# A planned Mamba and MLP kernel: joint silu groups, PSUM copies first, earlier fronts and new tie-breaks

## The chip, the cores and the metric

The kernel runs on one core of a Trainium2 chip. The metric is the device time of one execution in microseconds, as the median of several runs. The engines are TensorE (PE, with its weight loads as PEld), VectorE (DVE), ScalarE (ACT), GpSimd (POOL) and SyncE (SP), which here issues nearly all transfers between HBM and the on-chip memory SBUF. Matmuls write to PSUM, and another engine has to copy their results out.

## The reference

The input x is 8 samples of 384 channels by 32 x 32 pixels, so 1024 tokens of 384 channels per sample, all in float32. One layer has two halves:

```python
# for each of 8 samples, t: [1024, 384]
t  = layernorm(layernorm_over_channels(x))
xz = t @ in_proj_w.T                       # 384 -> 1536
xm, z = split(xz, 2)
xc = silu(causal_conv3(xm) + conv_b)       # 768 channels, 3 taps
dt, Bm, Cm = split(xc @ x_proj_w.T, [24, 40])
dt = softplus(dt @ dt_proj_w.T + dt_proj_b)
h_l = exp(dt_l * A) * h_{l-1} + dt_l * xc_l * Bm_l     # state: 768 x 16
y_l = (h_l . Cm_l) + xc_l * D
t  = (y * silu(z)) @ out_proj_w.T          # 768 -> 384
t  = gelu(t @ mlp_w1.T + b1) @ mlp_w2.T + b2           # 384 -> 1536 -> 384
x  = x + t
# then a feed-forward part on samples 0 to 4 (one group each of five)
h  = gelu(quant(layernorm(x) @ sign(W1 - mean).T + b1))
x  = x + quant(h @ sign(W2 - mean).T + b2)
```

`quant` scales a sample to 8 bits by its largest magnitude and clips it. The weights of the feed-forward part are binarised by groups of output features. For samples 5 to 7 that part is zero.

## The kernel before

**Tiling.** Features stand on the 128 partitions and tokens run along the free axis, in two halves of 512 (`HALVES`). For each sample there are four stages, written as functions of the class `Layer`:

- `s1(b)` is called the front. It loads x, normalises it (`norm`), projects it to xc (`p_in`, 6 x 3 matmuls per half), adds the three taps of the convolution from PSUM, applies silu, makes `p_dbc`, `p_all` and `p_dt`, applies softplus to dt, multiplies dt and xc, stores xc, dt, their product and B, C to HBM, and last projects the gate z (`p_z`) and applies silu to it (`gate`).
- `s2(b)` is the scan. Twelve tiles per sample, each with 4 groups of 4 states: ScalarE makes `da` = exp(dt A) into one of two PSUM buffers, GpSimd multiplies the input by B (`u<-dtx_r,bc`), VectorE runs the recurrence (L967), GpSimd or VectorE multiplies by C, and TensorE sums over states (`py`, L907). Samples 0 and 7 are scanned by halves, the others whole.
- `s3(b)` is the out-projection (`p_out`) and the MLP (`p_h`, gelu, `p_o`), per half.
- `ffn(b)`, for samples 0 to 4, is the binarised feed-forward part (`p_y`); `binarise` prepares its weights once.

**Buffers.** SBUF and PSUM tiles come from rings with a fixed number of buffers (L408 to L425). All matmuls but `py` write to the ring "mm" with three PSUM buffers. xc, z and dt of a front share the ring "front" with seven; the hidden layers share "hid" with nine.

**What sets the order.** No instruction is issued where it is written. `write_down` records operations with their costs, reads and writes in a `Plan`; `Plan.run` then plays a list scheduler: it keeps for each engine the time at which it is free, takes the engine that can start first, chooses one of its ready operations (`choose`) by rank (`rank`), emits it, and adds its cost. Each engine executes what it was given in that order, and semaphores between the engines follow from reads and writes. So the costs written in the code (`MM`, `c_act`, `c_dve`, the `cost` of each `add`, the `land` of a transfer) only set the order; on the chip, operations take what they take.

The rank (L295) puts `py` first (lane -1), then the scan (lane 0), then fronts of the samples up to `max(scanned + 1, FRONTS)` (lanes 1, 4, 11, 14), then the rest, then later fronts. On VectorE and GpSimd, stages go ahead of scans once they are ready (L287). Within a rank, the order of writing decides, shifted by up to 16 places through a hash (`turned`) of one number per 100 us of planned time from the table `TURNS` (L89).

ScalarE has a table of functions that must be loaded (`ACT_TABLE_LOAD`) before a function of another set. exp, silu, softplus and gelu need loads between them here; copies and scaled copies need none. `choose` stays with the loaded table as long as an operation of it is ready, unless it is exp (L283). To keep a function's operations together, the first operation of a group (`in_place`, L670; `gelu`, L1067) reads all tiles of the group, so none starts before all are there.

A copy out of PSUM (`affine`, L562) is planned on ScalarE, and VectorE may take it when it would start earlier. Where the planner sees TensorE idle for more than 0.7 us, it emits dummy matmuls `spare` of 128x256 (L350) as long as an "mm" buffer is free.

Of the kernel before, what the change touches and what calls it, by code (L numbers as in the profile page):

```python
# [33 lines left out]
P = 128  # L34
# [37 lines left out]
MM = 0.86  # L72
SWITCH = 0.26
BATCH = 2
# [3 lines left out]
EARLY = 2  # L78
FRONTS = 3
PATIENCE = 0.0  # L80
SLACK = 1.4
HOST = 0.3
NEAR = 1.0
LEAN = 1.1
LOAD_TABLE = 1.29


STRETCH, REACH = 100, 16
TURNS = (  # L89
    19522, 59978, 49910, 0, 34827, 0, 6565, 14275, 0, 7565, 33371, 19911,  # L90
    57895, 25116, 28986, 13399, 22123, 50761, 24784, 16788, 35300, 27386, 48162, 5457,
    0, 0, 40719, 11435, 20253, 0, 2806, 25936,
)


def turned(n, by):
# [3 lines left out]
    return (x ^ x >> 13) % (2 * REACH + 1) - REACH  # L100


def c_act(n):
    return 0.25 + n * 0.00084


def c_dve(n):
    return 0.19 + n * 0.00102


def c_pair(n):
    return 0.19 + n * 0.00188


def c_pool(n):
    return 0.18 + n * 0.00214

# [81 lines left out]
class Plan:  # L199
# [12 lines left out]
    def add(self, engine, cost, emit, r=(), w=(), claim=(), table=None, size=0, others=None,  # L212
            land=1.6):
        op = Op()
        op.engine, op.cost, op.emit, op.table = engine, cost, emit, table
        op.others, op.settle = others or {}, None
        op.size, op.land, op.prio = size, land, (*self.prio, len(self.ops))
        op.next, op.ready, op.tiles = [], 0.0, []
# [39 lines left out]
    def run(self):  # L258
# [7 lines left out]
        left, scanned = len(self.ops), 0  # L266

        def taken_by(op):
            return [t for t in op.tiles if t.ring is not None and t.real is None]
# [11 lines left out]
        def choose(e, now, able):  # L281
            able = [op for s, op in able if s <= now]
            if e == "ACT":  # L283
                same = [op for op in able if op.table == table and table != "exp"]
                plain = [op for op in able if op.table in (None, "exp")]
                able = same if table is not None and same else plain or able
            if e in ("DVE", "POOL"):  # L287

                able = [op for op in able if op.prio[0] > 0 and op.ready <= now - PATIENCE] or [
                    op for op in able if op.prio[0] == 0] or able  # L290
            at = int(now / STRETCH)
            turn = TURNS[at] if at < len(TURNS) else 0
            return min(able, key=lambda op: rank(op, turn))

        def rank(op, turn):  # L295


            lane, b = op.prio[:2]
            if lane <= 0:
                first = (lane, b)  # L300
            elif lane == 7:
                first = (EARLY, b)
            elif lane in (1, 4, 11, 14):
                first = (1, b) if b <= max(scanned + 1, FRONTS) else (3, b)
            else:
                first = (2, b)
            return (*first, op.prio[2] + (turned(op.prio[2], turn) if turn else 0))

# [12 lines left out]
        while left:  # L321
# [45 lines left out]
            if op.table is not None and op.table != table:  # L367
                cost += LOAD_TABLE
                table = op.table
            end = free[e] = clock.run(now, cost) if e == "PE" else now + cost  # L370
            if e == "SP":
                dma_free = max(dma_free, end + 0.5) + 0.05 + op.size / 360e3
                end = dma_free + op.land
# [17 lines left out]
class Layer:  # L391
# [115 lines left out]

    def load(self, to, view, src, r=(), size=0, cost=0.46, land=2.3):

        self.plan.add(  # L510
            "SP", cost, lambda: self.nc.sync.dma_start(view(to.real), src), r=r, w=[to],
            size=size, land=land,
        )
# [8 lines left out]
    def rows_moved(self, t, parts, move, r, w):  # L522
        n = P // len(parts)
        for i, mem in enumerate(parts):
            self.plan.add(
                "SP", 0.42, lambda i=i, mem=mem: move(t.real[i * n : (i + 1) * n, :], mem),
                r=r, w=w(i), size=4 * n * T,
            )

    def weights(self, ring, k, src, r=()):  # L530
        w = self.piece(ring, [P, k, P], ring)
        self.load(w, lambda t: t, src, r=r, size=4 * P * k * P, cost=0.37, land=1.5)
        return w
# [28 lines left out]
    def affine(self, out, in_, r, w, bias=0.0, scale=1.0, n=T, pool=False):  # L562
# [19 lines left out]
        if pool:  # L582
            others = {"POOL": (0.18 + n * 0.00095, on(nc.gpsimd))}
        else:
            others = {"DVE": (c_dve(n), on(nc.vector))}
        extra = 0.0 if plain else 0.09 if isinstance(scale, float) else 0.18
        self.plan.add("ACT", 0.16 + n * 0.00083 + extra, on_act, r=r, w=w, others=others)

    def norm(self, t, eps, scale):

        nc, add = self.nc, self.plan.add
        def columns(src, name):
# [10 lines left out]

            add("PE", 0.9, emit, r=[src], w=[p])
            return p

        def spread(src, name, turned=False):
# [29 lines left out]
        p_turned = self.piece("mm", [P, G], "p_turned")  # L637
        add("PE", 0.5, lambda: nc.tensor.matmul(
            p_turned.real, var.real, self.ident[:, ::DQ], start=True, stop=True
# [3 lines left out]
            r=[p_turned], w=[rstd])  # L643
        add("POOL", 0.8, lambda: nc.gpsimd.tensor_tensor(
            rstd.real, rstd.real, self.power.to_broadcast([P, G]), ALU.pow
# [8 lines left out]
    def s1(self, b):  # L654
# [14 lines left out]

        def in_place(t, func, table):  # L670
            parts = [t[k] for k in range(KD)]
            for p, piece in enumerate(t.pieces):
                mine = parts[p * PER : (p + 1) * PER]
                self.act(lambda piece=piece: piece.real, lambda piece=piece: piece.real, func,
                         c_act(PER * T), r=parts if p == 0 else mine, w=mine, table=table)
# [14 lines left out]
        def gate(half, t):  # L690
            z = self.split(r_z, KD, "z")
            for m in range(KD):
# [4 lines left out]
                )  # L697
            in_place(z, AF.Silu, "silu")
            by_pair("z", half, z)

        for half, cols in enumerate(HALVES):
# [4 lines left out]
            for m in range(KD):  # L706
# [12 lines left out]
                for s in (1, 2):  # L719
                    add("DVE", c_dve(T) + 0.06, lambda m=m, xc=xc, pm=pm, s=s, tap=tap: (  # L720
                        nc.vector.scalar_tensor_tensor(
# [4 lines left out]
            if half:  # L726
# [6 lines left out]

                add("POOL", 0.9, edge, r=[halo[m] for m in range(KD)], w=[self.edged])
                for p, piece in enumerate(xc.pieces):
                    add("POOL", 0.25, lambda p=p, piece=piece: nc.gpsimd.tensor_add(
                        piece.real[:, :, :2], piece.real[:, :, :2],
                        self.edge[:, p * PER : (p + 1) * PER, :2],
                    ), r=[self.edged], w=[piece[k] for k in range(PER)])
            all_m = [xc[m] for m in range(KD)]  # L740
            in_place(xc, AF.Silu, "silu")
            by_pair("xc", half, xc)


# [12 lines left out]

            add("PE", 0.26 + KC * MM, low, r=[w, *all_m], w=[p_dbc], claim=[dbc])
            self.affine(lambda dbc=dbc: dbc.real, lambda p_dbc=p_dbc: p_dbc.real, [p_dbc], [dbc])
# [12 lines left out]
            for k in range(0, KD, 2):  # L772
# [16 lines left out]
                for i in range(2):  # L789
# [3 lines left out]
                    )  # L793
            in_place(dt, AF.Softplus, "softplus")
            d = self.dram["dtx", b]
# [8 lines left out]
            for p, piece in enumerate(dt.pieces):  # L804
# [5 lines left out]
                )  # L810
            gate(half, t)

# [13 lines left out]
    def scan(self, b, half, state):  # L826
# [7 lines left out]

        def load(to, view, src, r, size):
            self.plan.add("SP", 0.57, lambda: nc.sync.dma_start(view(), src), r=r, w=[to],  # L836
                          size=size, land=2.3)

        def quad_rows(i):
            r = self.piece(f"bc{i}", [P, n], f"bc{i}")  # L840
            src = rows.real[i * SQ : (i + 1) * SQ, cols].unsqueeze(0).to_broadcast([DQ, SQ, n])
            load(r, lambda: r.real, src, [rows[h] for h in halves], 4 * P * n)
            return r
# [90 lines left out]
    def scan_pair(self, u, cols, n, dts, dtxs, bq, cq, state, half, on_pool):  # L934
# [14 lines left out]
        for t, mine in enumerate(cols):  # L949
            da = self.piece("da", [P, wide, n], "da")  # L950
            dt_r = dts[t]
            for i, col in enumerate(mine):
                self.act(
                    lambda i=i, da=da: da.real[:, i, :],
                    lambda i=i, dt_r=dt_r: dt_r.real[:, i, :], AF.Exp,
                    0.26 + n * 0.00084, r=[dt_r[i]], w=[da], table="exp",
                    scale=self.a_neg[:, col : col + 1],
# [43 lines left out]
    def s3(self, b):  # L1001
        nc, a, add = self.nc, self.a, self.plan.add
        yg_d = self.dram["yg", b]
        for half, cols in enumerate(HALVES):
# [12 lines left out]
            else:  # L1017
                yg = self.split("hid", KD, "yg")
                for p, piece in enumerate(yg.pieces):
# [5 lines left out]
                        w=[piece[k] for k in range(PER)], claim=yg.pieces[p:],  # L1025
                        size=4 * P * PER * T, land=2.3,
                    )
# [12 lines left out]
            for h in range(KH):  # L1040
# [5 lines left out]
                )  # L1046
                if h % HK == HK - 1:
                    self.gelu(g, h + 1 - HK)
            for m in range(KC):
                rows = slice(m * P, (m + 1) * P)  # L1050
                res = self.piece("res", [P, T], "res")

                self.load(res, lambda t: t, a["x"][b, rows, cols], r=[g[HK]], size=4 * P * T)
                po = self.mlp_out(lambda i, m=m: a["mlp_w2"][m, i], "w6", g, [res], "p_o")
# [11 lines left out]

    def gelu(self, g, k0, r=(), **kw):  # L1067
        parts = [g[k] for k in range(k0, k0 + HK)]
        for i in range(0, HK, PER):
            piece = g.pieces[(k0 + i) // PER]  # L1070
# [129 lines left out]
    def clip(self, view, n, parts, q):  # L1200
        self.plan.add("POOL", 0.13 + n * 0.0009, lambda: self.nc.gpsimd.tensor_scalar(
            view(), view(), q.real[:, 2:3], q.real[:, 1:2], ALU.min, ALU.max
        ), r=[q], w=parts)

    def ffn(self, b):
# [32 lines left out]
        for h, cols in enumerate(HALVES):  # L1238
            g = self.split("hid", KH, "gf")
            for p, piece in enumerate(g.pieces):  # L1240
# [3 lines left out]
                    r=[y1_d[h, p * PER + m] for m in range(PER)], w=parts,  # L1244
                    claim=g.pieces[p:], size=4 * P * PER * T, land=2.3)
                self.clip(lambda piece=piece: piece.real, PER * T, parts, q1)
# [135 lines left out]
```

## Time and profile before

| | |
|---|---|
| median of 3 runs | 3187.56 us (3181.11 to 3189.2) |
| the profiled execution | 3184.62 us, of which the span of instructions 3182.5 us |
| TensorE busy, idle | 3083.4, 99.1 us |
| dummy matmuls `spare` | 58.1 us (114 matmuls, two records each) |
| granted TensorE clock, mean | 0.988 |
| VectorE, ScalarE, GpSimd busy | 2644.0, 1966.5, 2744.8 us |
| table loads of ScalarE | 172 profiled (173 in the program), 1283 ns each |
| `p_h` matmuls | 1152 records for 576 matmuls of 128x512, 511.7 us busy |
| copies of 128x512 out of PSUM | 583 to 775 ns on ScalarE, 681 to 801 ns on VectorE |

How to read the rows that follow. A row of stretches gives first the stretch and its length, then busy microseconds and number of instructions of PE, PEld, DVE, ACT and POOL, then the granted clock, the busy share of the DMA engines and GB/s. A row of waits names the engine and instruction that waited, after the arrow the one that released it, and then the total in us, how often, and the longest. A row of a group names line, engine, operation, tiles, count, busy us and mean ns of one, and then the idle time of its engine just before it.

The span ends with 66 us in which only the MLP of the last half is left; before that the last scan has to be done. Sample by sample, the last `py` ends at 531, 917, 1301, 1664, 2035, 2395, 2755 and 3113 us.

### The profile page before, as it was taken

The numbers are of one execution on the slowest core, as the hardware profiler recorded it, in microseconds if no ns is written. First come the engines' busy times: TensorE is split into PE (matmuls) and PEld (weight loads), VectorE is DVE, ScalarE is ACT, GpSimd is POOL, SyncE is SP. The second block draws the span as 40 slices with busy tenths as digits, with TensorE's granted clock in tenths as the row PEclk, the third lists the DMA queues.
The fourth block names the chain that finished last, engine by engine and source line by source line (L and its number), as shares of the span: only waits on it lengthen the run. The fifth ranks groups of instructions, "written<-read, shape, count | busy, mean of one in ns | idle before, by whom it ended". The sixth has DMA issues, their size and how long they took to land. (4 is left out here: it accounts for less than half of the span.)

```text
span 3182.5 us, 33759 instructions
## 1 busy us (share of the span) xinstructions
PE 3083.4 (97%) x10972; PEld 1274.9 (40%) x10972; DVE 2644.0 (83%) x2081; ACT 1966.5 (62%) x2363; POOL 2744.8 (86%) x1046
## 2 busy tenths in 40 slices
PE   9898999999999999999999999999999999999999
PEld 4333434343433443433444434343434443433334
DVE  4697888899788798879998888889789987888881
ACT  4777786855665556665656655666566555655552
POOL 1788889988988978999979999799989999998980
PEclk9998999999989999999999999999999999999999
DMA  7797789757786667875696766877677856756542
GB/s 231 261 310 263 252 261 329 255 195 259 239 283 221 198 227 254 295 250 185 230 319 234 252 207 232 298 236 254 219 257 254 282 196 213 235 175 209 160 148 72
DMA packets 348975, 751.85 MB, mean 236 GB/s; under 512 B 36481, under 2 KB 113793, under 8 KB 339585
## 3 DMA queue, kind: packets, MB, share of 16 engines
q1 hardware_dynamic: 348368, 749.61, 71.0%
q8 instruction: 88, 1.44, 0.2%
q14 instruction: 87, 0.70, 0.1%
q10 hardware_dynamic: 432, 0.09, 0.0%
HBM read 569.21 MB, written 180.36 MB: 236 GB/s over the span
## 5 line engine op out<-in xcount | busy, mean ns | idle before, releaser
L942 POOL TENSOR_TENSOR u<-dtx_r,bc 128x2048 f32<-128x2048 f32 (+1 forms) x360 | 1185.5, 3308 | 124.9 <-PE py L907 79.7
L556 ACT ACTIVATE da<-dt_r,a_neg 128x1024 f32<-128x1024 f32 (+1 forms) x960 | 900.5, 945 | 490.0 <-DVE u L967 272.3
L942 POOL TENSOR_TENSOR u<-u,bc 128x2048 f32<-128x2048 f32 (+1 forms) x274 | 900.1, 3290 | 86.9 <-DVE u L967 81.4
L967 DVE TENSOR_TENSOR_SCAN u<-da,u 128x1024 f32<-128x1024 f32 (+1 forms) x436 | 869.1, 2007 | 127.1 <-POOL u L942 71.4
L540 PE MATMUL p_h<-t,w_b 128*128 128x512 f32 x1152 | 511.7, 597 | 10.8 <-DMA w_b<-in_mlp_w 6.8
L540 PE MATMUL p_o<-g,w 128*128 128x512 f32 x1152 | 512.6, 597 | 5.1 <-DMA w<-in_mlp_w 5.1
L967 DVE TENSOR_TENSOR_SCAN da<-da,dtx_r 128x1024 f32<-128x1024 f32 (+1 forms) x192 | 386.3, 2019 | 55.6 <-POOL dtx_r L942 34.2
L942 POOL TENSOR_TENSOR dtx_r<-dtx_r,bc 128x2048 f32<-128x2048 f32 (+1 forms) x120 | 396.8, 3311 | 2.4
L540 PEld LDWEIGHTS p_h<-t,w_b 128*128 128x128 f32 x1152 | 214.0, 190 | 298.0 <-issue 257.7
L540 PEld LDWEIGHTS p_o<-g,w 128*128 128x128 f32 x1152 | 214.3, 190 | 295.8 <-issue 277.9
L540 PE MATMUL p_y<-tn,w_b 128*128 128x512 f32 x720 | 319.6, 597 | 2.2 <-DVE tn L648 2.2
L540 PE MATMUL p_y<-gf,w_n 128*128 128x512 f32 x720 | 320.3, 597 | 0.8 <-ACT gf L556 0.5
L907 PE MATMUL py<-u,fold 128*32 128x512 f32 x2304 | 303.5, 628 | 0.2 <-POOL u L942 0.2
L967 DVE TENSOR_TENSOR_SCAN da<-da,u 128x1024 f32<-128x1024 f32 (+1 forms) x140 | 283.7, 2041 | 13.7 <-POOL u L942 6.9
L540 PE MATMUL p_out<-yg,w 128*128 128x512 f32 x552 | 245.6, 597 | 4.2 <-DMA w<-in_out_proj_last 1.5
L540 PE MATMUL p_z<-t,w_f 128*128 128x512 f32 x504 | 233.4, 610 | 9.2 <-DMA w_f<-in_in_proj_w 5.1
L540 PE MATMUL p_in<-t,w_f 128*128 128x512 f32 x504 | 229.7, 601 | 5.6 <-DMA w_f<-in_in_proj_w 3.7
L556 ACT ACT_TABLE_LOAD x172 | 220.7, 1283 | 3.1
L540 PEld LDWEIGHTS p_y<-gf,w_n 128*128 128x128 f32 x720 | 133.9, 190 | 185.3 <-issue 173.8
L540 PEld LDWEIGHTS p_y<-tn,w_b 128*128 128x128 f32 x720 | 134.0, 190 | 182.1 <-issue 165.1
L571 ACT ACTIVATE g<-p_h,v_vecs 128x512 f32<-128x512 f32 x158 | 107.7, 684 | 145.2 <-PE p_h L540 144.7
L571 ACT ACTIVATE y<-p_y,v_vecs 128x512 f32<-128x512 f32 x138 | 94.2, 684 | 166.9 <-PE p_y L540 139.0
(132 smaller groups left out, 3245.0 us busy)
## 6 DMA issues: line engine op xcount, KB each, us to landing
dt_r<-dt_d SPq DMA_DIRECT2D x144, 512.0 KB, 5.5
dtx_r<-dtx_d SPq DMA_DIRECT2D x72, 1024.0 KB, 6.0
w_b<-in_mlp_w SPq DMA_DIRECT2D x192, 192.0 KB, 3.1
w<-in_mlp_w SPq DMA_DIRECT2D x96, 384.0 KB, 3.5
w_f<-in_in_proj_w SPq DMA_DIRECT2D x168, 192.0 KB, 4.8
y_d<-y SPq DMA_DIRECT2D x120, 256.0 KB, 4.7
gf<-y_d SPq DMA_DIRECT2D x60, 512.0 KB, 6.9
xc_d<-xc SPq DMA_DIRECT2D x48, 512.0 KB, 5.6
```

The source lines that it names most:

```text
L540: self.nc.tensor.matmul(p.real, w.real[:, w0 + k, :], t.at(k0 + k), start=start and k == 0, stop=stop and k == n - 1,)
L556: lambda: self.nc.scalar.activation(out(), in_(), func, **{k: v() if callable(v) else v for k, v in kw.items()}),
L571: nc.scalar.activation(out(), in_(), AF.Identity, bias=bias, scale=scale)
L907: nc.tensor.matmul(py.real[g * DQ : (g + 1) * DQ, :], self.fold, hc, start=False, stop=(q == NQUAD - 1), skip_group_check=True,)
L942: nc.gpsimd.tensor_mul(u.real[:, x], t.real[:, x], row.real.unsqueeze(2).to_broadcast([P, n, 2]))
L967: da=da, in_u=in_u: nc.vector.tensor_tensor_scan(to(i), da.real[:, i, :], in_u(i), state.real[:, col : col + 1] if half else 0.0, ALU.mult ...
```

## The change

Five things change.

- **Joint silu.** For samples 2 to 7 (`JOINT`) the gate's projection is written right behind the convolution, and one group of silu covers xc and z: six operations, the first of which reads all twelve parts. The z stores follow the xc stores. For samples 0 and 1 the gate stays last.
- **gelu by eight and four.** In `s3`, the twelve hidden tiles get gelu in groups of 8 and 4 tiles where they had two of 6.
- **PSUM first.** When at most one buffer of "mm" is free (`SCARCE`), ScalarE chooses among the operations that touch one, if there are any that need no other table.
- **Fronts.** `FRONTS` is 4 where it was 3.
- **Costs, ties and flags.** Most costs are set anew, ScalarE and VectorE count as free 0.09 and 0.08 us before an operation's end (`LAG`), transfers get rates by kind. `TURNS` has 30 new numbers, and four bits of each may let fronts wait (`LATE_FRONTS`), scans go first on VectorE or GpSimd (`DVE_SCANS`, `POOL_SCANS`) or stages go first on ScalarE (`ACT_STAGES`) in that stretch of 100 us.

```diff
-SWITCH = 0.26
+SWITCH = 0.22
+JOINT = range(2, B)
-FRONTS = 3
+FRONTS = 4
+SCARCE = 1
+LATE_FRONTS, DVE_SCANS, POOL_SCANS, ACT_STAGES = 1 << 16, 1 << 17, 1 << 18, 1 << 19
 TURNS = (
-    19522, 59978, 49910, 0, 34827, 0, 6565, 14275, 0, 7565, 33371, 19911,
...
+    17610, 24087, 20212, 39788, 55575, 59023, 81989, 22321, 58617, 812894,
+    311620, 51673, 560357, 59520, 80314, 2104, 50573, 559844, 6159, 58063,
+    51278, 41401, 6390, 863060, 0, 672911, 34250, 39179, 27191, 131575,
 )
+LAG = {"ACT": 0.09, "DVE": 0.08}
 def c_act(n):
-    return 0.25 + n * 0.00084
+    return 0.2 + n * 0.00084
...
         def choose(e, now, able):
             able = [op for s, op in able if s <= now]
+            at = int(now / STRETCH)
+            turn = TURNS[at] if at < len(TURNS) else 0
             if e == "ACT":
                 same = [op for op in able if op.table == table and table != "exp"]
                 plain = [op for op in able if op.table in (None, "exp")]
                 able = same if table is not None and same else plain or able
+                if turn & ACT_STAGES:
+                    able = [op for op in able if op.prio[0] > 0 and op.table in (None, "exp")] or able
+                if len(self.spare.ring.free) <= SCARCE:
+                    able = [op for op in able if self.spare.ring in map(ring_of, op.tiles) and (
+                        op.table in (None, "exp", table))] or able
             if e in ("DVE", "POOL"):
-                able = [op for op in able if op.prio[0] > 0 and op.ready <= now - PATIENCE] or [
-                    op for op in able if op.prio[0] == 0] or able
+                scans = [op for op in able if op.prio[0] == 0]
+                if not (turn & (DVE_SCANS if e == "DVE" else POOL_SCANS) and scans):
+                    able = [op for op in able if (
+                        op.prio[0] > 0 and op.ready <= now - PATIENCE)] or scans or able
+                else:
+                    able = scans
...
             elif lane in (1, 4, 11, 14):
-                first = (1, b) if b <= max(scanned + 1, FRONTS) else (3, b)
+                soon = 2.5 if turn & LATE_FRONTS else 1
+                first = (soon, b) if b <= max(scanned + 1, FRONTS) else (3, b)
...
-            end = free[e] = clock.run(now, cost) if e == "PE" else now + cost
+            end = clock.run(now, cost) if e == "PE" else now + cost
+            free[e] = end - LAG.get(e, 0.0)
             if e == "SP":
-                dma_free = max(dma_free, end + 0.5) + 0.05 + op.size / 360e3
+                dma_free = max(dma_free, end + 0.4) + op.size
...
-            others = {"DVE": (c_dve(n), on(nc.vector))}
+            others = {"DVE": (c_dve(n) + (0 if isinstance(scale, float) else 0.15), on(nc.vector))}
...
-        def in_place(t, func, table):
-            parts = [t[k] for k in range(KD)]
-            for p, piece in enumerate(t.pieces):
+        def in_place(func, table, *ts):
+            parts = [t[k] for t in ts for k in range(KD)]
+            for p, piece in enumerate(piece for t in ts for piece in t.pieces):
...
-            in_place(xc, AF.Silu, "silu")
+            z = gate(half, t) if b in JOINT else None
+            in_place(AF.Silu, "silu", *([xc, z] if z else [xc]))
             by_pair("xc", half, xc)
+            if z:
+                by_pair("z", half, z)
...
-            gate(half, t)
+            if not z:
+                z = gate(half, t)
+                in_place(AF.Silu, "silu", z)
+                by_pair("z", half, z)
...
-                if h % HK == HK - 1:
-                    self.gelu(g, h + 1 - HK)
+                if h in (7, 11):
+                    self.gelu(g, 0 if h == 7 else 8, n=8 if h == 7 else 4)
```

The other hunks set costs of single operations (the norm's matmuls from 0.9 to 0.78, the clip from 0.13 + 0.0009 n to 0.2 + 0.00096 n, and the like).

## The prediction

> **What bounds the kernel now.** I read the page's busy shares first, then its slices, then the stretches of 100 us, then the waits, and last the length of each sample's scan.
>
> ```profile
> PE 3083.4 (97%) x10972; PEld 1274.9 (40%) x10972; DVE 2644.0 (83%) x2081; ACT 1966.5 (62%) x2363; POOL 2744.8 (86%) x1046
> ...
> PE   9898999999999999999999999999999999999999
> ...
> POOL 1788889988988978999979999799989999998980
> PEclk9998999999989999999999999999999999999999
> ```
>
> TensorE is busy for 97% of the span, so only what it loses can be won: 3182.5 - 3083.4 = 99.1 us idle; the dummy matmuls `spare`, 58.1 us; and the clock, granted at 0.988, so 0.012 x 3182.5 = 38 us. Together 195 us; some 2987 us are real work that the change leaves as it is. The stretches show where the loss lies (columns: stretch, its length, then busy us and instructions of PE, PEld, DVE, ACT, POOL, granted clock, DMA share, GB/s):
>
> ```profile
> 100.00:200.00 100.00, 86.70 (x323) 35.08 (x322) 86.75 (x88) 80.56 (x116) 93.00 (x66) 0.95 0.83 278
> 200.00:300.00 100.00, 80.56 (x316) 29.10 (x315) 85.67 (x93) 74.42 (x111) 85.09 (x57) 0.87 0.80 267
> ...
> 900.00:1000.00 100.00, 92.44 (x318) 37.59 (x317) 78.92 (x57) 63.13 (x71) 94.06 (x33) 0.90 0.75 250
> ...
> 2200.00:2300.00 100.00, 99.94 (x319) 39.01 (x318) 84.79 (x58) 64.18 (x70) 98.59 (x34) 1.00 0.76 250
> ```
>
> The first three stretches hold 12.4 + 13.3 + 19.4 = 45 us of the idle time, and the first four 23 us of the clock's loss. 900 to 1000 holds 7.6 and 10 us. From 1000 to 2700 TensorE loses 15 us in all, and GpSimd is nearly as full. The same by sample (from the first scan to the last `py` of each of the eight samples; samples 0, 2, 3, 6 are shown):
>
> ```profile
> 70.00:531.00 461.00, 416.31 (x1559) 169.35 (x1557) 376.05 (x376) 349.04 (x495) 388.94 (x230) 0.95 0.83 277
> ...
> 917.00:1301.00 384.00, 374.15 (x1333) 154.49 (x1330) 325.39 (x231) 231.53 (x262) 336.13 (x97) 0.97 0.72 239
> 1301.00:1664.00 363.00, 359.70 (x1284) 148.16 (x1283) 320.89 (x224) 215.18 (x238) 331.69 (x99) 1.00 0.73 246
> ...
> 2395.00:2755.00 360.00, 358.25 (x1239) 153.05 (x1238) 316.53 (x227) 211.01 (x230) 340.97 (x107) 1.00 0.71 236
> ```
>
> Sample 0 takes 461 us, samples 1 and 2 386 and 384, the later ones 358 to 371. GpSimd works 332 to 341 us of each of samples 3 to 6 and idles 19 to 31: there little can be won by any order. So there are two bounds, TensorE in the first 1300 us and both engines after it, and the gain has to come from samples 0 to 2.
>
> **The change, part by part.** No arithmetic changes: the new program has the same real matmuls, scans, products and 2255 DMAs; what differs is order, who empties PSUM, table loads (173 to 195) and dummies (114 to 109).
>
> *One silu group for xc and z (samples 2 to 7), gelu by eight and four.* The first should take ScalarE loads away: groups that start with z fall from 15 to 4. But `LAG` lets ScalarE choose 0.09 us before its last operation ends, and the second operation of a group depends on the end of the first, which read all its parts. At that moment it cannot be chosen, so an exp or a PSUM copy can slip in and split the group. The built order shows it: gelu loads 31 to 43, those that start with xc 16 to 20, softplus 16 to 19, feed-forward gelu 11 to 12, returns to exp 83 to 96.
>
> ```profile
> L556 ACT ACT_TABLE_LOAD x172 | 220.7, 1283 | 3.1
> ...
> DVE u L967 <- ACT da L556: 62.4, 47, 5.8
> ...
> DVE da L967 <- ACT da L556: 26.6, 22, 6.7
> ```
>
> By this row 22 loads are 22 x 1.283 = 28.2 us. The Trainium skill speaks against the change here: "ScalarE: Activation LUTs", What ACT_TABLE_LOAD costs, puts 1380 ns of drain beside the 1283 ns of each switch, and its Table sets section says to batch by set; 22 x 2.66 would be 58.5 us. The row shows 3.1 us of idle time before 172 loads, so no such drain; I take 28. ScalarE idles 3182.5 - 1966.5 = 1216 us, which hides most. What shows is VectorE waiting for exps: 62.4 + 26.6 = 89 us over 83 returns, 1.07 us each. 13 more returns give 14 us; VectorE is 83% busy and some of that is covered: +10 us, bounds 0 and 28. Queued behind a load on ScalarE stand the next exp, and behind that VectorE's scan, GpSimd's product and `py`. The split gelu wins nothing at the very end: in the chain 72 `p_o` follow 72 `p_h` without a gap. The joint group makes `p_dbc` wait for six more projections, 18 x 0.888 (511.7 us over 576 `p_h`, two records each) = 16 us later per half. Samples 2 to 7 stand well ahead of their scan, which hides it; without that cover a scan would start 16 us late. The z stores go before the `p_dbc` weights in SyncE's queue, three of 0.59 us (the issue of an xc store in the timeline): 1.8 us, under the same cover. Both 0.
>
> *PSUM emptied first.* With one or no "mm" buffer free, ScalarE prefers an operation that frees one. TensorE's own waits behind such copies:
>
> ```profile
> PE p_all L762 <- ACT dbc L569: 4.2, 1, 4.2
> ...
> PE p_dbc L752 <- ACT halo L569: 3.7, 1, 3.7
> PE p_dt L783 <- ACT dbc L569: 2.7, 3, 1.6
> PE p_mean L616 <- ACT mean L571: 2.6, 6, 0.5
> PE p_mean L616 <- ACT dt L571: 2.5, 2, 1.7
> PE p_in L540 <- ACT dt L571: 2.4, 3, 0.8
> ```
>
> With five smaller rows for copies of halo, dt, z, g and var (2.1, 2.3, 2.0, 2.1, 2.1) and `p_all` behind dbc on VectorE (1.5) this is 18.1 + 12.1 = 30 us. I take two thirds: -20 us, bounds 0 and -30. The copy that goes ahead delays an exp by its 0.58 to 0.68 us; scans then wait, already in the +10. ScalarE also takes over copies: 85 of 128x512 (z, dt, g, xc, y, t) are left on VectorE of 112. 27 x 0.74 = 20 us less on VectorE, 27 x 0.68 = 18 us more on ScalarE; both have idle time, 0.
>
> *Four early fronts.* In the order, by the last `py` of sample 0 TensorE has done 372 full 128x512 matmuls where it had done 344, and 38 dummies for 49. By sample 1 the lead is 39 matmuls, by sample 2 16, by sample 7 none. So 28 x 0.888 = 25 us of real work is drawn into the holes of sample 0, and taken out of sample 2. This is worth the holes that it fills. Of the 45 us idle before 300 us, about 15 are start-up data (first x, norm, the `p_sums` weights) that no order fills; PSUM-first already took about 15 there; I give this part the remaining 15: -15, bounds 0 and -20. Dummies: (109 - 114) x 0.51 (58.05 over 114) = -2.5. The clock follows idle time in this trace: each of the longer half-speed stretches in its record (131, 223, 250, 264, 295, 919 us) stands right behind waits. If the waits shrink by the above, I take 15 of the first 23 us and 5 of the 10 at 919: -20, bounds 0 and -33. If nothing is there to hide the front (the drawn work itself has to wait for its weights), it costs its 25 us in sample 0.
>
> *The planner's costs, ties and flags.* They only re-order. Waits for weights (`p_sums` 6.8, `p_h` 6.8, `p_o` 5.1, `p_z` 5.1, `p_in` 3.7 and 2.0, `p_out` 1.5 and 0.8) are 32 us; transfers are now costed finer, kind by kind. No row says how much better: bounds -20 and +10, taken -5. Flags let scans or stages go first, or fronts later, in nine stretches of 100 us: 0.
>
> *What is given back.* Where GpSimd is full, TensorE's saved time turns into waiting. The order carries as many dummies late (47 in samples 6 and 7 before, 51 after: 2 us). I take +8, bounds 0 and 25.
>
> Sum: +10 - 20 - 15 - 2.5 - 20 - 5 + 8 = -44.5 us. The profiled execution has a span of 3182.5 us and a time of 3184.6; the median of the runs is 3187.6, 5.1 above the span. Span 3138.0, so the time 3143 us.
>
> **The rivals.**
> - *Given back.* The early holes close, but samples 3 to 7 are set by GpSimd and cannot run faster than their 358 to 371 us, while exps come later: only samples 0 to 2 gain, 30 us, and 12 go again: 3170. For it: 19 us of GpSimd idle in samples 5 and 6. Against: 31 in samples 3 and 4.
> - *Deep gain.* Nearly all PSUM, weight and early waits go and the clock stays up: -30 - 20 - 33 - 15 - 2.5 + 10 = -90: 3097. For it: every term is idle time in the trace. Against: sample 1 carries more real work than before.
> - *Nothing happens.* The new order has its own waits of the same size, as its almost equal number of dummies suggests: 3187, within 0.3% (9.6 us, about what a measurement can tell).
> - *Slower: the table loads decide.* From sample 3 on, each extra return to exp stalls the loop exp, scan, product, as GpSimd has no slack: the whole 28 us, and the early gain stays under 15 us since the drawn fronts delay sample 0. It decides once a return costs over 2 us instead of 1.07 and the holes give less than that: 3187 + 28 - 5 = 3210. For it: more loads, and 62 us of VectorE waiting on exps. Against: most loads stand in ScalarE's 1216 us idle.
>
> **How the numbers follow.** Main case 0.50 (its own range 3115 to 3170), deep gain 0.17, given back 0.17, nothing 0.08, slower 0.08. Faster 0.50 + 0.17 + 0.17 = 0.84, same 0.08, slower 0.08. The range reaches from below the deep gain to just past "nothing": 3085 to 3190; it leaves out the slower case and the tail of the deep one.
>
> **What would show it.** TensorE's idle time from 99 to about 60 us, that of the first 300 us from 45 to about 20; granted clock from 0.988 to 0.994 or more; about 194 table loads and more VectorE waiting on `da`; the last `py` of sample 0 near 515 us, of sample 2 near 1265 (1301 before), samples 3 to 7 within 10 us of their lengths. Wrong would be: idle time over 85 us, a clock still at 0.988, or samples 3 to 7 longer by over 5 us each.

## The result, and the profile after

The changed kernel takes 3153.12 us in the median (3150.01 to 3154.6) beside 3188.38 us for the kernel before on the same chip: 35 us less, a ratio of 0.989 with a 95% interval of 0.9868 to 0.9911. The profiled execution has a span of 3152.0 us where it had 3182.5; that is 30.5 us less, where single executions of the kernel before lie between 3181.11 and 3193.61 us. One execution of the run `more_loads` was in a slow state (5717 us at a granted clock of 0.745), and all times below are of fast runs.

The page of the changed kernel, busy shares and slices:

```profile
PE 3073.8 (98%) x10962; PEld 1274.0 (40%) x10962; DVE 2602.0 (83%) x2056; ACT 2000.8 (63%) x2409; POOL 2747.2 (87%) x1047
...
PE   9989999999999999999999999999999999999999
...
POOL 1788888998999988999989999989998999988990
PEclk9999999999999999999999999999999999999999
```

TensorE is idle for 3152.0 - 3073.8 = 78.2 us (99.1 before) and its clock is granted at 0.992 in the mean (0.988), so the clock costs 0.008 x 3152 = 25 us (38). The dummies last 58.9 us, though there are five fewer (58.1). Taking the dummies out, TensorE is busy for 3073.8 - 58.9 = 3014.9 us where it was 3025.3, with the same 10744 records of matmuls: I put the 10.4 us down to the higher clock. So the 30.5 us of the span are 20.9 us of idle time and 10.4 us of clock, less 0.8 us of dummies.

The stretches of 100 us that stood out, in the changed kernel (the columns are those of the rows before the change):

```profile
100.00:200.00 100.00, 90.10 (x347) 36.31 (x346) 81.10 (x85) 83.01 (x115) 82.57 (x58) 0.97 0.88 296
200.00:300.00 100.00, 92.35 (x392) 37.61 (x391) 82.83 (x91) 84.72 (x125) 85.77 (x59) 0.95 0.89 299
...
900.00:1000.00 100.00, 99.55 (x383) 39.01 (x382) 86.50 (x58) 68.16 (x78) 96.79 (x27) 1.00 0.83 291
```

From 200 to 300 TensorE is busy for 92.4 us instead of 80.6 and its clock is at 0.95 instead of 0.87; from 900 to 1000 it is busy for 99.6 us instead of 92.4, and the slow clock there is gone. In the first 300 us 45 us of idle time became 28. By sample, with the ends of the last `py` of this trace:

```profile
70.00:550.00 480.00, 448.29 (x1727) 184.67 (x1729) 383.54 (x387) 382.12 (x541) 389.48 (x234) 0.98 0.86 287
550.00:929.00 379.00, 373.04 (x1422) 155.80 (x1414) 336.05 (x253) 245.70 (x285) 346.18 (x111) 1.00 0.74 252
929.00:1287.00 358.00, 353.46 (x1333) 146.26 (x1327) 318.76 (x232) 230.44 (x258) 331.26 (x99) 0.99 0.76 257
1287.00:1652.00 365.00, 361.59 (x1278) 148.27 (x1278) 311.36 (x217) 221.68 (x240) 340.68 (x102) 0.99 0.70 239
1652.00:2010.00 358.00, 356.60 (x1234) 145.17 (x1234) 310.88 (x223) 220.46 (x241) 336.61 (x105) 1.00 0.72 244
2010.00:2380.00 370.00, 367.41 (x1254) 149.78 (x1242) 316.03 (x229) 238.81 (x258) 340.15 (x105) 1.00 0.74 248
2380.00:2726.00 346.00, 342.05 (x1172) 144.97 (x1168) 298.62 (x209) 199.20 (x215) 337.44 (x103) 1.00 0.70 229
2726.00:3082.00 356.00, 343.25 (x1066) 136.99 (x1062) 294.13 (x263) 213.28 (x306) 315.69 (x176) 0.99 0.55 170
```

The samples of the kernel before that the prediction leaves out (1, 4, 5 and 7):

```profile
531.00:917.00 386.00, 375.25 (x1418) 154.10 (x1414) 341.99 (x259) 245.29 (x273) 342.95 (x113) 0.99 0.74 250
...
1664.00:2035.00 371.00, 366.02 (x1340) 150.02 (x1336) 321.17 (x231) 228.03 (x247) 339.60 (x108) 1.00 0.71 238
2035.00:2395.00 360.00, 359.03 (x1229) 145.78 (x1226) 311.69 (x222) 228.42 (x251) 340.77 (x106) 1.00 0.75 251
...
2755.00:3113.00 358.00, 345.50 (x1068) 136.87 (x1066) 294.88 (x263) 207.24 (x301) 316.43 (x176) 1.00 0.56 171
```

Sample 0 got longer, 480 us for 461, with 32 us more TensorE work in it; samples 1 and 2 lost 7 and 26. Samples 3 to 7 went from 363, 371, 360, 360, 358 to 365, 358, 370, 346, 356: 17 us less together. In sample 6 GpSimd is busy for 337 of 346 us.

Where a sample got shorter is not where the time was won. In samples 3 to 7 TensorE is busy for 1770.9 us instead of 1788.5, 17.6 us less, and idle for 24.1 us instead of 23.5: it has less work there and wastes as much. Of the full 128x512 matmuls, 28 more than before are done by the end of sample 0, 16 more by the end of sample 2 and none more at the end; at 0.888 us each those 16 are 14 of the 17.6 us. In the same way sample 2 has 20.7 us less of TensorE's work. TensorE's idle time fell in samples 0, 1 and 2, by 13.0, 4.8 and 5.3 us.

Some of TensorE's waits on PSUM copies, then the table loads and VectorE's waits on exps:

```profile
PE p_all L785 <- ACT dbc L590: 1.9, 3, 1.2
PE p_mean L637 <- ACT mean L592: 1.9, 3, 0.7
PE p_in L561 <- ACT dt L592: 1.6, 2, 0.8
```

```profile
L577 ACT ACT_TABLE_LOAD x194 | 248.9, 1283 | 3.5
...
DVE u L993 <- ACT da L577: 70.3, 56, 5.1
...
DVE da L993 <- ACT da L577: 28.4, 27, 2.5
```

`p_all` waits 1.9 us for dbc (4.2 before), the wait of `p_dbc` for halo (3.7) is gone. I grouped TensorE's waits by what the releasing instruction did. Behind one that reads a PSUM tile it waited 26.7 us on ScalarE and 25.2 on VectorE before, 11.9 and 20.9 after: 19 us less. Behind transfers it waited 32.2 and now 24.5. But behind ScalarE's other operations (exps, silus, gelus, squares), which read no such tile, it waited 3.4 us and now 10.5: 7 us of what the copies won went back there. VectorE waits 70.3 + 28.4 = 98.7 us for exps, where it waited 89.0.

### The profile page after: what moved, and what is told of

It is laid out like the page before. It is cut to its first block, busy times and chain, and to the rows that moved or that the text cites. A ratio compares the mean times of both kernels' runs of the same rounds, so it can differ in the third digit from the quotient of the medians.

```text
span 3152.0 us, 33796 instructions
## 1 busy us (share of the span) xinstructions
PE 3073.8 (98%) x10962; PEld 1274.0 (40%) x10962; DVE 2602.0 (83%) x2056; ACT 2000.8 (63%) x2409; POOL 2747.2 (87%) x1047
## 4 chain that ended last, share of the span: by engine, by line
PE 72%; DVE 7%; DMA 7%; ACT 6%; POOL 5%; issue 3%; SPq 1%; DVEq 0%; POOLq 0%; ACTq 0%
PE p_y L561 15%; PE p_o L561 14%; PE p_h L561 14%; PE py L933 9%; PE p_out L561 6%; PE p_in L561 5%; PE p_z L561 5%; POOL u L968 3%; DVE u L993 2%; DVE da L993 2%; ACT da L577 2%; DMA dtx_r<-dtx_d 1%; ACT L577 1%; PE p_dt L806 1%; DMA w<-in_out_proj_w 1%
## 5 line engine op out<-in xcount | busy, mean ns | idle before, releaser
L561 PE MATMUL p_h<-t,w_b 128*128 128x512 f32 x1152 | 518.3, 603 | 11.5 <-DMA w_b<-in_mlp_w 6.9
```

The source lines that it names most:

```text
L561: self.nc.tensor.matmul(p.real, w.real[:, w0 + k, :], t.at(k0 + k), start=start and k == 0, stop=stop and k == n - 1,)
```

## The experiments

Every run is compared with the kernel before on the same chip, whose median was 3187.8 to 3190.2 us. Edits are cut to the lines that matter (`...`). Three questions: what a table load costs, where the gain of 35 us comes from, and whether the parts can be told apart.

**More table loads, in the same order.**

```diff
+            if table == "exp":
+                self.exps += 1
+                if self.exps % 36 == 0:
+                    self.nc.scalar.activation(self.scrap, self.one, AF.Silu)
...
```

> The changed kernel in the same order on every engine, but before every 36th exp of the scan ScalarE runs a one-column silu that nobody reads: 26 more returns to exp, 51 more table loads, 51 x 1.283 = 65 us more on ScalarE. My theory (1.07 us of VectorE waiting per return, of which about seven tenths reach the end): +20 us, 3173. The rival 'table loads decide' (each load lies fully in the scan's loop): +65 us and more, 3218. Hidden altogether: 3153.

3178.2 us, ratio 0.9961 (0.9947 to 0.9975). That is 25 us above the changed kernel by the medians and (0.9961 - 0.989) x 3190 = 23 us by the ratios: 0.9 to 1.0 us for each of the 26 added silus with its return to exp, of the 2.6 us that two loads last. So more than half of an added load is hidden, and neither extreme holds. What waited in this run is not shown.

**No dummy matmuls.**

```diff
-                    self.fill()
+                    pass
```

> The changed kernel in the same order without the 109 dummy matmuls (they are planned, but not emitted). Theory: they only fill time in which TensorE would wait, and keep the clock up at the start and around 300 and 2500 us; without them the granted clock falls from 0.992 to about 0.985 and the time rises by 5 to 25 us. If they cost what they last (0.5 us each), the time falls by up to 50 us.

3158.3 us, 0.9893 (0.9879 to 0.9908). The granted clock of its profile is 0.985 in a span of 3159.1 us:

```profile
PE 3047.1 (96%) x10744; PEld 1241.2 (39%) x10744; DVE 2602.1 (82%) x2056; ACT 2000.9 (63%) x2409; POOL 2746.7 (87%) x1047
```

By the medians this is 5 us, at the lower end of the theory, and by the intervals no difference from 0.989. The same matmuls took 3047.1 us instead of 3014.9, 32 us more. The time in which TensorE had none of them to do fell from 78.2 + 58.9 = 137.1 us to 3159.1 - 3047.1 = 112.0, 25 us less. So most of those 32 us fell into time in which TensorE would otherwise have waited or run dummies.

**Both kernels with an empty table.** The cut shows the changed kernel.

```diff
-TURNS = (
-    17610, 24087, 20212, 39788, 55575, 59023, 81989, 22321, 58617, 812894,
...
-)
+TURNS = ()
```

> The changed kernel with an empty table: no shifts of ties and no flags, the structure, the rules and the costs stay. If the gain of 35 us lies in structure, rules and costs, this stays near 3153 to 3165; if it lies in the table, it goes back to 3185 or above.

> The kernel before with an empty table. If the old table was worth as much as the new one, this is as far above 3188 as the changed kernel with an empty table is above 3153 (some 10 to 30 us), and the difference between the two without tables is what structure, rules and costs give: about 35 us by my sum, 0 if the table alone makes the gain.

3244.3 us, 1.0165 (1.0152 to 1.0178), and 3251.1 us, 1.0186 (1.0169 to 1.0203). So the new table is worth 91 us to its kernel and the old one was worth 61 to 63 to the other. Without tables the two are 7 us apart (0 to 13 by the two intervals, an estimate). My sum had put nearly the whole gain into the written parts and 5 us into the re-ordering; here the written parts, rules and costs show about 7 of 35 us unless the table exploits them. The four flags stand in the table too, so this does not tell what they give from what the shifts of ties give.

**Fresh tables of equal effort.** An empty table is only one order. So I chose a table for each variant in the same way: going through the stretches, the best of 32 random entries by the end of the kernel's own plan. The plan's end serves only to choose; all times are from the chip. The edits below leave out the new numbers of `TURNS`.

> The changed kernel with another table: chosen afresh, stretch by stretch, as the one of 32 random entries that ends the plan earliest. It is the yardstick for the next three, whose tables are chosen in the same way with the same effort. Between 3160 and 3230 us: below 3244 (empty table), and above 3153 unless any table of this kind serves as well.

3186.8 us, 0.9987 (0.9977 to 0.9998). Much better than the empty table, 34 us short of the table that the change brought.

> fresh_full with other random numbers for its table, chosen in the same way with the same effort; the plan ends 8.5 us earlier than that of fresh_full. It shows how far two tables of equal effort lie apart on the chip: under 8 us if the plan's end tells the time, up to 20 if it tells little; a difference of fresh_plain from fresh_full below that spread then says nothing on the written parts.

3207.9 us, 1.0068 (1.0055 to 1.0081). The same code with another table of the same effort is 21 us slower, although its plan ends 8.5 us earlier. So the plan's end does not rank orders at this distance, and 21 us is the spread against which single parts must be read.

```diff
-JOINT = range(2, B)
+JOINT = ()
```

> As fresh_full, with the joint silu group undone alone (the gate last in every sample). 234 table loads, 14 returns to exp more: 14 us above fresh_full if the joint group counts by its loads; 0 or below if its gain is eaten by the longer wait of p_dbc for six more projections.

3190.5 us, 1.0 (0.9988 to 1.0012): 4 us above fresh_full, inside the spread.

```diff
-SCARCE = 1
+SCARCE = -1
```

> As fresh_full, with the preference for PSUM copies undone alone. By my sum +20 us over fresh_full, with TensorE waiting longer behind copies out of PSUM (40.7 us in fresh_full); within the spread of tables if a fresh order makes up for the rule.

3187.4 us, 0.9996 (0.9985 to 1.0006): 1 us above fresh_full. TensorE waits 43.9 us behind readers of PSUM (40.7 in fresh_full); behind those on ScalarE, which the rule is about, it waits 22.0 us without the rule and 25.8 with it. My 20 us for this rule are not seen in this comparison.

```diff
-JOINT = range(2, B)
+JOINT = ()
-FRONTS = 4
+FRONTS = 3
-SCARCE = 1
+SCARCE = -1
-                if h in (7, 11):
-                    self.gelu(g, 0 if h == 7 else 8, n=8 if h == 7 else 4)
+                if h % HK == HK - 1:
+                    self.gelu(g, h + 1 - HK)
```

> As fresh_full, with all four written parts undone: the gate stays last in every sample, gelu by six and six, no preference for PSUM copies, three early fronts; costs, LAG and a fresh table stay. 252 table loads, so 24 returns to exp more than fresh_full: +24 us by the loads alone, and +20 for PSUM copies by my sum: 44 us above fresh_full. If the written parts do nothing and order alone counts: within 10 us.

3196.6 us, 1.0019 (1.0011 to 1.0027): 10 us above fresh_full and 11 below fresh_full_b. Neither the 44 us of my sum, nor proof that the parts do nothing.

```diff
-                same = [op for op in able if op.table == table and table != "exp"]
+                same = [op for s, op in every if (
+                    s <= now + 0.1 and op.table == table and table != "exp")]
...
```

> As fresh_full, but an operation of the loaded function counts as ready 0.1 us early, so that groups on ScalarE stay whole: 148 table loads where fresh_full has 205. At the 1.0 us per return to exp that more_loads showed, 28 returns fewer are worth 28 us less than fresh_full. If loads are hidden when they stand in real groups, it is within 10 us of it.

3169.1 us, 0.9931 (0.9913 to 0.995), with 147 loads in its profile: 18 us below fresh_full and 39 below fresh_full_b. This hints that whole groups are no loss when the whole order is planned for them; with one table it is a hint. Its count also speaks for `LAG` as what splits the groups: the other five fresh tables give 202 to 252 loads.

**Whole groups in the changed kernel's own order.** If loads cost 1.0 us per return, healing the split groups should win 22 us.

```diff
+    def together(self, ops):
+        emits = [op.emit for op in ops]
+        for op in ops:
+            op.emit = lambda: None
+        ops[0].emit = lambda: [emit() for emit in emits]
...
```

`together` is called on the operations of each silu, softplus and gelu group.

> The changed kernel with the same order on TensorE, VectorE, GpSimd and SyncE; on ScalarE the operations of a silu, softplus or gelu group are issued right behind the first one, where the plan had let exps or PSUM copies slip between. 151 table loads for 195, 22 returns to exp fewer, 44 x 1.283 = 56 us less on ScalarE. At the 1.0 us per return that more_loads showed: 22 us less than the changed kernel, 3131, ratio to the kernel before 0.982. If the exps and copies that now stand behind a whole group (2 to 5 us) cost as much as the loads did: 3153, ratio 0.989.

3178.6 us, 0.997 (0.9959 to 0.9981): 25 us slower than the changed kernel, with 44 loads fewer. Table loads, waits of VectorE on exps and of TensorE on copies in this kernel:

```profile
L577 ACT ACT_TABLE_LOAD x150 | 192.4, 1283 | 2.7
```

```profile
DVE u L1002 <- ACT da L577: 75.4, 49, 8.2
...
DVE da L1002 <- ACT da L577: 52.3, 29, 5.9
```

```profile
PE p_all L794 <- ACT dbc L596: 4.3, 1, 4.3
...
PE p_in L561 <- ACT xc L598: 3.8, 2, 2.5
```

VectorE waits 127.7 us for exps instead of 98.7, in fewer and longer waits (8.2 us the longest, it was 5.1). TensorE waits 22.3 us behind ScalarE's reads of PSUM instead of 11.9 and 27.4 behind VectorE's instead of 20.9, 17 us together, and 29.6 behind transfers instead of 24.5; `p_all` waits 4.3 us in one piece again. So the 56 us that ScalarE saves are outweighed by what waits longer.

**Copies may slip in, exps wait.** Which of the two costs?

```diff
+            if table == "exp":
+                while self.pending:
+                    self.pending.pop(0)()
...
```

`pending` holds the rest of a group that has begun; it is issued before the next exp.

> As groups_together, but a PSUM copy may still slip into a group where the plan put it; only an exp waits, until the group is done. 151 table loads as there, the other engines' order is the changed kernel's. If groups_together was 25 us slow because copies stood behind groups, this is at 3153 or, with the loads saved, near 3135. If the exps that stand behind the groups are what costs, it stays near 3178.

3171.9 us, 0.995 (0.9934 to 0.9966), and its waits:

```profile
DVE u L1012 <- ACT da L579: 74.9, 47, 8.2
DVE da L1012 <- ACT da L579: 53.2, 28, 5.9
```

VectorE's wait for exps stays at 128.1 us; the waits behind ScalarE's PSUM reads fall from 22.3 to 15.6. So by the medians 7 of the 25 us go with the copies, though the two intervals overlap (0.995 against 0.997), and 19 us remain with the exps delayed. In this order the loads saved do not make up for the exps that come late. What these two runs cannot separate is a group's own delay from any departure of one engine from an order that was chosen for all five. Part of the loss may be that alone.

No version that I tried beats the changed kernel.

## Why the prediction was right, point by point

The time of 3153 us lies in the range (3085 to 3190) and in the main case's own range (3115 to 3170); the forecast was 3143. The wide range held "nothing happens" (3187) as well, so it is the main case that was tested.

- *TensorE bounds the kernel, and the gain is idle time and clock.* Right: 20.9 + 10.4 us of the 30.5. The idle terms of the sum (+10, -20, -15, -5, +8) made -22; measured -20.9. That they meet so closely is in part luck: +8 was not needed, 7 us behind ScalarE's other operations had no term of their own, and the parts behind the terms are not shown one by one.
- *PSUM first, -20.* The waits behind readers of PSUM fell by 19 us, as summed: 14.8 on ScalarE, which the rule is about, and 4.3 on VectorE. Of the 30 us that I counted, 7.9 stood behind VectorE's copies (dt, z, g, dbc), which the rule does not touch. But the rule by itself is not shown as the cause: undone with a fresh table it makes 1 us, and 3 us of these waits. The term had the right size for the whole order and was given to one rule.
- *Weights, -5.* The waits behind transfers went from 32.2 to 24.5: -7.7.
- *Table loads, +10.* VectorE's waiting on exps rose by 9.7 us, as worked out from 1.07 us per return, and the added loads cost 0.9 to 1.0 per return. The drain at each switch of which the Trainium skill speaks ("ScalarE: Activation LUTs", What ACT_TABLE_LOAD costs) is not in this trace: 3.5 us of idle time before 194 loads, and 8.0 us behind them. Its rule to batch by set (Table sets) made the kernel slower where the rest of the order was kept, as groups_together shows; with a table chosen for whole groups, fresh_whole was faster than both fresh tables with split ones, so the rule is not refuted. That was the part I missed: I booked the splits as a cost alone. They also let copies and exps pass, and in this order that is worth more.
- *Fronts, -15, and sample 0 ending near 515 us.* The sample ended at 550. 32 us more busy time went in and 13 us of idle time out, so 19 us were lost there; sample 2 then gave back 26, of which 20.7 are work that had been done earlier, ending at 1287 where I had 1265. The 13 us are near the 15, but a single cause for them is not shown.
- *Clock, -20.* It measured -10 to -13: 0.992, not 0.994. New half-speed stretches of 6.8 and 10.2 us near 1272 and 1593 us took 8.5 us of it. This is one of the two largest errors of the sum, but of one execution: the other three were granted 0.993 to 0.995.
- *Given back, +8, as GpSimd is full.* Not needed: TensorE's idle time in samples 3 to 7 rose by 0.6 us, and they became 17 us shorter, as part of TensorE's work there had been done before. I was right that the idle time would be won in samples 0 to 2, and wrong that GpSimd holds the later ones to their length: an order that keeps it busy for 337 of 346 us exists, against 341 of 360 before. I read 19 us of its idle time as the floor; it was at most 9.
- *Dummies, -2.5.* +0.8: five fewer, but slower ones.
- *From span to median, +5.* It was 1 us. This and the smaller gain of the span (30.5 for 44.5) make the 10 us.

The step that failed in its reasoning, though the time came out near, is "They only re-order", with -5. With empty tables the kernels are 7 us apart and with their tables 35: the new table is worth 28 to 30 us more to its kernel than the old one to its own. The parts that I costed one by one look more like places where a better order shows than like separate causes. How much each is worth alone stays open: two tables of equal effort are 21 us apart, more than the 4, 1 and 10 us that undoing parts made. So does whether the shifts of ties, the flags or the new costs carry the gain; none was undone with the rest of the order kept.

## What to carry to other kernels

When a scheduler writes the order, cost the change by idle time and clock of the engine that bounds, as a whole; what single rules give need not add up, and an undone rule must be compared with the spread between orders of equal effort. When work moves between stages, compare the idle time of the bounding engine by stage, not the length of the stage. Before joining operations to save a table load, look at what would wait behind the joined group: a load of 1.28 us that lets an urgent copy or exp pass can be the cheaper one, as long as the rest of the order stays. An engine's idle time in one order is not its floor.

## What the runs showed of the hardware

A table load that is added in front of an exp stream costs 0.4 to 0.5 us of the end-to-end time here (23 to 25 us for 51 loads), not 1.283 us; ScalarE is busy for 63% of the span. And a lower granted clock did not cost what its mean says: without dummies the mean fell from 0.992 to 0.985, which is 22 us of full-speed work, and the time rose by 5 us, as 25 us of waits and dummies went away at the same time.
